# A graph layer on one core: slots of 511 rows in four blocks instead of 383 in three, and a longer gather list

## The chip, the cores and the metric

The kernel runs on one core of one Trainium2 chip. The metric is the device time of one execution in microseconds (us). Five engines with queues of their own work in it: TensorE (PE; its weight loads are listed apart as PEld), VectorE (DVE), ScalarE (ACT), GpSimd (POOL) and SyncE (SP), which only issues DMAs here. Before the change the median of three runs is 703.79 us (703.43 to 704.61).

## The reference

6250 nodes have 256 features each, 100,000 edges run from node `src` to node `dst` and are sorted by `dst`. Cut to what matters:

```python
theta_x = (x[dst] - x[src]) @ theta_w.T + theta_b
phi_x = x[src] @ phi_w.T + phi_b
e = relu(theta_x + phi_x)
out = segment_max(e, dst, num_segments=6250)     # nodes without edges: 0
return layernorm(x + out)
```

Since the maximum runs over the edges of one node, the part that depends on `dst` leaves the maximum: with B = x @ (phi_w − theta_w).T a node needs the largest B row of its sources, column by column; to it come x @ theta_w.T and the biases, then the relu, the sum with x and the normalisation.

## The kernel before, in words

**B.** PE computes B for all nodes in pairs of 128 rows (`b_of`, L782 to L794) and ACT writes it to `b_rows` in DRAM. `weights` holds both matrices, [:, :, 0] for B and [:, :, 1] for theta.

**Two parts.** The first 618 nodes (part 1) are served by gathers alone: 81 steps (`FIRST_STEPS`), in each of which GpSimd gathers one row of B for each of the 128 partitions by an indirect DMA (`gather`, L527 to L535), and DVE takes the running maximum (`run_steps`, L687 to L707; line L696). Steps go in groups of 8, on a ring of 5 tiles named `g`. The first two groups (`X_GROUPS`) gather rows of x and need no `b_rows`; the others wait for it. The other 5632 nodes (part 2) are 44 (`TILES`) in each partition, with room for 36 (`R`) edges each, their ranks.

**Slots.** The rows of B are cut into slots of 383 rows (`SLOT_ROWS`), two blocks of 128 (`KB` = 3 blocks with the last) and one of 127; the free row holds a very small value for "no edge here". There are 17 slots, of which the last has 122 rows and so one block. For each slot and node one edge is chosen whose source lies in the slot (`choice`, L1027 to L1055, on DVE, two slots at a time, int16 over `CHOICE_R` = 24 ranks); its row number within the slot goes to `chosen_rows` in DRAM (`wanted`). Rows are then fetched by products with one-hot matrices: for each slot and each chunk of 1024 nodes (`CHUNKS`, five of 1024 and one of 512), `make_hots` (L1144 to L1161) loads the row numbers to all partitions and builds one one-hot block of 128 x 1024 for each block of rows. ACT does it in two passes, |want − row| (L1157) and relu(1 − that) (L1160); DVE does a block in one (L1155): the first block in each slot's first chunk and, once `dve_hots` is set, the first in every chunk. `slot_halves` (L1099 to L1140) multiplies: B is split into two float32r terms (`slot_terms`, L1071 to L1095), each chunk has two halves of 128 features, each half blocks x 2 terms x 2 matmuls of 512 columns (L1120) into a PSUM tile of two banks, `ps_f`, of which there are three. ACT copies the halves of slot 0 into `acc` (L1132), DVE takes the maximum of `acc` and the halves of all other slots (L1134, the evictions).

**The list.** What the slots do not choose (a second edge of the same node and slot, and ranks past the 24th) is put into a list of 128 x 256 places (`LIST_CHUNK`): `list_pieces` (L1247 to L1322) marks the edges that are left, moves them to the front of each partition in 11 steps of DVE (L1278, L1288), stores them in `list_words` in DRAM, and reads them back by three indirect DMAs (`gather_run`, L540 to L544), so that each partition has 256 steps whatever node they belong to. Each step is a gather of `b_rows` (`gather_2`) and a maximum (L696) as in part 1; the last is a carry. The groups are stored to `maxima_2`, and at the end each node's maximum is gathered from there by its place (44 gathers).

**What sets the order.** GpSimd's gathers have a written order (`in_turn`). While the list is built, the loop at L1555 hands out by turns the groups of part 1 (even pieces) and parts of slots (odd pieces), with `AHEAD_OF_RUNS` chunks behind the store and one fewer behind the reads. In the list (L1606 to L1632) the steps of group i − 2 stand between the gathers of group i; every second gather waits for a step of DVE that lies 16 steps back (`hold`, L537). `halves_until` (L1601) spreads the slots' halves over the list, but for the last 10 chunks (`LAST_CHUNKS`), which come behind it. DVE's evictions are tied to the list's steps by order-only dependencies (L1139), so that both run in this order. Within these ties a scheduler places the instructions of each engine.

**The end.** `rows_of` (L1359 to L1420) handles the nodes in shares of 8, 4 and 2 tiles: theta's products, the transposed `acc`, the gathered maxima, relu, sum and normalisation. The first share stands between the last chunks of the last slot (L1657).

A `pause` of one iota of 160 elements stands behind each `gather_run` and behind the gather of the heads of part 1 (L544, L928). If a window, the list or a partition does not hold the data, `flags` makes the kernel run `general_path` behind the rest.

Of the kernel before, what the change touches and what calls it, by code (L numbers as in the profile page):

```python
# [39 lines left out]
FP = mybir.dt.float32  # L40
# [11 lines left out]
P = 128  # L52
# [17 lines left out]
PAUSE = 160  # L70
CHOICE_R = 24
# [11 lines left out]
LAST_CHUNKS = 10  # L83
LEAD = 2
STEPS_BITS = 3
OWN_LIST = 316
LIST_CHUNK = 256
# [348 lines left out]
def gnn_kernel(ctx: ExitStack, tc: tile.TileContext, x, src, dst, theta_w, theta_b, phi_w, phi_b, out):  # L436
# [14 lines left out]
    CW = 1024  # L451
# [4 lines left out]
    assert D == 2 * P and LEFT1 > 0 and OWN % 512 == 0 and TILES < 64 and P * T1 < E and WINDOW < E  # L456
    assert (P - 1) * T + 1 < E <= P * T and N < ID_MASK and P * T <= EDGES and E + 8 * P <= EDGES
    assert SLOT * NS <= slot_code(WORD - 1) < 1 << 15 and N < WORD and WORD << TABLE_BITS == 1 << 23 and SLOT == 1 << SLOT_BITS and P == 1 << P_BITS and SLOT_ROWS < SLOT and KB == 3 and ROWS == P - 1 and WINDOW <= 8 * P and OWN_LIST * P < 1 << 20
    BATCH_S = 2
    assert STEPS == 1 << STEPS_BITS and 3 * BATCH_S * CHOICE_R * TILES // 2 + TR <= 6 * WINDOW and LIST_CHUNK + 1 == LIST and LIST_CHUNK % STEPS == 0 and 3 * (BACK + LIST_CHUNK) <= WINDOW and BACK == R - 2 and CARRY_GROUPS * STEPS >= BACK and BACK + LIST_CHUNK <= OWN_LIST and R == 36 and CHOICE_R == 24 and OWN_LIST <= 512 and 1536 < TR <= 1536 + OWN_LIST  # L460
# [47 lines left out]
    pause = const.tile([P, PAUSE], FP, name="pause")  # L508
# [211 lines left out]
    weights = const.tile([P, KC, 2, D], FP, name="weights")  # L720
# [3 lines left out]
    with (  # L724
# [6 lines left out]
        w_in = prep.tile([P, 2, KC, D], FP, name="w_in")  # L731
        for i, w in enumerate((phi_w, theta_w)):
            nc.sync.dma_start(w_in[:, i], w.rearrange("(c p) k -> p c k", p=P))
        biases = prep.tile([P, 2, D], FP, name="biases")
        nc.vector.tensor_sub(w_in[:, 0], w_in[:, 0], w_in[:, 1])
        for i in range(2):
            for c in range(KC):
# [3 lines left out]
                weights_made = nc.vector.tensor_copy(weights[:, :, i, c * P : (c + 1) * P], ps[:, 0])  # L741
# [40 lines left out]
        def b_of(to, rows, kept=None):  # L782
# [6 lines left out]
            for h in range(n):  # L789
                for k in range(KC):  # L790
                    nc.tensor.matmul(  # L791
                        ps[:, h, :], x_t[:, h, k, :], weights[:, k, 0, :], start=(k == 0), stop=(k == KC - 1)
# [125 lines left out]
    def heads_1(capped):  # L918
# [4 lines left out]
        carried = work.tile([P, D], FP, name="carried", bufs=1)  # L923
# [4 lines left out]
        in_turn(iota(pause, 1, 0, 0))  # L928
# [13 lines left out]
    words, work_1, work_2, order = (table(n) for n in ("words", "work_1", "work_2", "order"))  # L942
# [5 lines left out]
    behind_in_order(iota(order, 1, 1, 0), windows_fetched[0], "runs ahead of the ranks")  # L948
# [78 lines left out]
    def choice(s0):  # L1027
# [71 lines left out]
    def slot_halves(s, c):  # L1099
# [13 lines left out]
        for h in range(KC):  # L1113
            ps = ps_fetch.tile([P, CW], FP, name="ps_f")
            ps = ps[:, :wide_of]
            n = blocks * PARTS
            for i in range(n):
                b, part = divmod(i, PARTS)
                for w in range(0, wide_of, 512):
                    one = nc.tensor.matmul(  # L1120
                        ps[:, w : w + 512],
                        terms[:, part, b, h * P : (h + 1) * P],
                        hot[:, b, w : w + 512],
# [6 lines left out]
            to = acc[:, h, begin : begin + wide_of]  # L1130
# [116 lines left out]
    def list_pieces():  # L1247
# [10 lines left out]
        nc.vector.tensor_tensor(up_to[:, 1:], node_ends(order), node_ends(before_it), op=ALU.subtract)  # L1258
# [7 lines left out]
        distance = order.bitcast(I32)  # L1266
# [37 lines left out]
        list_edges, second, third = (dst_w[:, i * n_run : (i + 1) * n_run] for i in range(3))  # L1304
# [54 lines left out]
    def rows_of(part, j0, n, ps_tile):  # L1359
# [18 lines left out]
        def piece(k):  # L1378
            w = min(2, n - k)
            if part == 2:  # L1380
                j = j0 + k
                if j % 4 == 0:
                    x_tiles[0] = kept_ring.tile([P, 4 * KC, P], FP, name="kept")
                    rows = x_columns[:, j * KC * P : (j + 4) * KC * P]
# [317 lines left out]
```

## Time and profile before

| | before |
|---|---|
| median of 3 runs | 703.79 us (703.43 to 704.61) |
| the profiled execution | 703.84 us, span 702.0 us, granted clock 0.97 |
| PE busy | 650.7 us (93%) |
| PEld busy | 532.1 us (76%) |
| DVE busy | 627.0 us (89%) |
| ACT busy | 513.2 us (73%) |
| POOL busy | 438.1 us (62%) |
| slot products (L1120) | 2156 matmuls, 508.1 us |
| list gathers (L528, list_src) | 256, 262.4 us |
| evictions (L1134) | 192, 216.4 us |

Times in rows of the profile are microseconds from the start of the span, unless a row gives a mean in ns. A row of a group of instructions has the line, the engine, the operation, tiles out<-in, shape, count, then busy time, mean ns of one, idle time of the engine ahead of them and what ended it. A row of the order of time has start, duration, engine, line, operation, and in brackets the idle time before it and what ended that. The span starts at the first and ends at the last instruction of the profiled execution.

### The profile page before, as it was taken

The page shows a single profiled execution, that of the slowest core. Times are in us where ns is not written, and L with a number is a line of the kernel's source. Part 1 is how long each engine was busy: PE and PEld are TensorE (multiplying, and loading weights), DVE is VectorE, ACT ScalarE, POOL GpSimd, SP SyncE. Part 2 cuts the span into 40 slices and gives each one's busy share as a digit, 9 for nine tenths or more (in the row PEclk, how much of TensorE's full clock was granted, in tenths as well). Part 3 has the DMA queues.
Part 4 walks back from the last instruction along what each step waited for, and adds up shares of the span by engine and source line. Part 5 has one row for each costly group of instructions (what it writes and reads, how often), then busy time and mean ns, then how long its engine had stood idle before and what let it go on. Part 6 is the DMA issues. An engine that isn't in the chain of part 4 may idle for free.

```text
span 702.0 us, 9583 instructions
## 1 busy us (share of the span) xinstructions
PE 650.7 (93%) x2908; PEld 532.1 (76%) x2908; DVE 627.0 (89%) x1200; ACT 513.2 (73%) x597; POOL 438.1 (62%) x424
## 2 busy tenths in 40 slices
PE   4899978879798999999999999999999999999991
PEld 3688866657577788888888888888888878888881
DVE  6999999999998778989889897889888898979996
ACT  1345668989888877868778786779877687863596
POOL 6800178888813757777777677777667776057720
PEclk9899989989999999999999999999999999999996
DMA  8898563656645747868697689788887776655775
GB/s 249 293 350 322 191 187 109 204 192 210 215 174 182 260 150 255 266 225 284 209 319 241 219 302 332 230 247 280 307 267 262 247 235 208 206 170 162 261 292 206
DMA packets 61308, 167.04 MB, mean 238 GB/s; under 512 B 11944, under 2 KB 21953, under 8 KB 55233
## 3 DMA queue, kind: packets, MB, share of 16 engines
q1 hardware_dynamic: 40005, 106.89, 43.9%
q0 software_dynamic: 18976, 52.35, 25.1%
q10 hardware_dynamic: 2268, 7.11, 2.8%
q8 instruction: 25, 0.41, 0.3%
q14 instruction: 34, 0.28, 0.1%
HBM read 102.94 MB, written 63.36 MB: 237 GB/s over the span
## 4 chain that ended last, share of the span: by engine, by line
PE 61%; DVE 16%; ACT 7%; POOL 6%; issue 5%; DMA 4%; ACTq 0%; SPq 0%; DVEq 0%; POOLq 0%
PE ps_f L1120 58%; POOL g L528 6%; DVE words L1005 2%; ACT hot L1157 2%; ACT x_f L1458 2%; ACT hot L1160 2%; DMA g<-b_rows,src 1%; DVE work L1002 1%; DVE g L696 1%; ACT squares L1443 1%; DVE wide L1038 1%; DVE x_f L1414 1%; PE ps_e L1400 1%; DMA dst_w<-in_dst_dram,window 1%; DVE g L1410 1%
## 5 line engine op out<-in xcount | busy, mean ns | idle before, releaser
L1120 PE MATMUL ps_f<-hot,terms 128*128 128x512 f32 x2156 | 508.1, 396 | 18.8 <-DVE hot L1155 10.5
L1120 PEld LDWEIGHTS ps_f<-hot,terms 128*128 128x128 f32 x2156 | 406.6, 190 | 113.8 <-ACT hot L1160 14.6
L528 POOL DMA_INDIRECT g<-b_rows,list_src x256 | 262.4, 1025 | 107.8 <-issue 52.2
L1157 ACT ACTIVATE hot<-want,minus_row 128x1024 fp32r<-128x1024 f16 (+1 forms) x214 | 219.3, 1074 | 99.1 <-PE ps_f L1120 98.9
L1134 DVE TENSOR_TENSOR acc<-acc,ps_f 128x1024 f32<-128x1024 f32 x192 | 216.4, 1129 | 49.7 <-PE ps_f L1120 47.8
L1160 ACT ACTIVATE hot<-hot 128x2048 fp32r<-128x2048 f32 (+2 forms) x102 | 188.8, 1851 | 2.4
L696 DVE SCALAR_TENSOR_TENSOR g<-g,caps 128x256 f32<-128x256 f32 x335 | 161.1, 481 | 1.7
L528 POOL DMA_INDIRECT g<-b_rows,src x65 | 92.3, 1420 | 66.5 <-DMA b_rows<-b_sb 47.1
L791 PE MATMUL ps_b<-weights,x_t 128*128 128x256 f32 x260 | 63.7, 400 | 7.6 <-ACT x_t L779 7.2
L528 POOL DMA_INDIRECT g<-maxima,place x44 | 42.2, 960 | 33.7 <-DMA maxima<-g 20.6
L791 PEld LDWEIGHTS ps_b<-weights,x_t 128*128 128x128 f32 x260 | 50.4, 200 | 16.7 <-ACT x_t L779 10.1
L1155 DVE TENSOR_SCALAR hot<-want,row_id 128x1024 fp32r<-128x1024 f16 x80 | 56.9, 712 | 0.0
L794 ACT COPY b_sb<-ps_b 128x512 f32<-128x512 f32 (+1 forms) x25 | 14.4, 579 | 30.8 <-PE ps_b L791 21.1
L1400 PE MATMUL ps_e<-weights,kept 128*128 128x256 f32 x144 | 34.0, 379 | 0.0
L1443 ACT ACTIVATE squares<-x_f,r 128x256 bf16<-128x256 f32 x47 | 23.2, 494 | 12.5 <-DVE r L1440 12.5
L1400 PEld LDWEIGHTS ps_e<-weights,kept 128*128 128x128 f32 x144 | 27.3, 190 | 3.6
L528 POOL DMA_INDIRECT g<-in_x_dram,src x16 | 21.1, 1320 | 5.4 <-issue 4.1
L779 ACT COPY x_t<-ps_xt 128x512 f32<-128x512 f32 (+1 forms) x33 | 18.3, 590 | 7.8 <-PE ps_xt L776 7.6
L1458 ACT ACTIVATE x_f<-x_f,r 128x256 f32<-128x256 f32 x40 | 20.6, 587 | 4.6 <-DVE r L1450 4.6
L1288 DVE COPY_PREDICATED work<-words,work 128x316 int32<-128x316 int32 (+9 forms) x11 | 18.2, 1659 | 0.0
L1414 DVE SCALAR_TENSOR_TENSOR x_f<-g,x_f 128x256 f32<-128x256 f32 x44 | 17.1, 423 | 0.3
L1038 DVE TENSOR_TENSOR wide<-wide 128x88 int16<-128x88 int16 (+5 forms) x45 | 16.2, 360 | 1.3
(273 smaller groups left out, 405.8 us busy)
## 6 DMA issues: line engine op xcount, KB each, us to landing
maxima<-g SPq DMA_DIRECT2D x41, 1024.0 KB
want<-chosen_rows SPq DMA_DIRECT2D x85, 256.0 KB
x_q<-in_x_dram SPq DMA_DIRECT2D x12, 512.0 KB
b_rows<-b_sb ACTq DMA_DIRECT2D x12, 512.0 KB
x_columns<-x_t SPq DMA_DIRECT2D x22, 256.0 KB
kept<-x_columns SPq DMA_DIRECT2D x11, 512.0 KB
raw<-b_rows SPq DMA_DIRECT2D x16, 256.0 KB
g<-b_rows,list_src POOLq DMA_INDIRECT x256, 4.9
```

The source lines that it names most:

```text
L528: one = nc.gpsimd.indirect_dma_start(out=to, out_offset=None, in_=table, in_offset=bass.IndirectOffsetOnAxis(ap=offsets, axis=0))
L696: one = nc.vector.scalar_tensor_tensor(g[:, k, :], last[part], caps[:, t : t + 1], g[:, k, :], op0=ALU.min, op1=ALU.max)
L791: nc.tensor.matmul(ps[:, h, :], x_t[:, h, k, :], weights[:, k, 0, :], start=(k == 0), stop=(k == KC - 1))
L1120: one = nc.tensor.matmul(ps[:, w : w + 512], terms[:, part, b, h * P : (h + 1) * P], hot[:, b, w : w + 512], start=(i == 0), stop=(i == n ...
L1134: one = nc.vector.tensor_tensor(to, to, ps, op=ALU.max)
L1155: nc.vector.tensor_scalar(hot[:, b, :], want, row_id[:, b : b + 1], None, op0=ALU.is_equal)
L1157: nc.scalar.activation(hot[:, b, :], want, AF.Abs, bias=minus_row[:, b : b + 1], scale=1.0)
L1160: nc.scalar.activation(apart, apart.bitcast(FP), AF.Relu, bias=1.0, scale=-1.0)
L1400: nc.tensor.matmul(a[:, i, :], x_t[:, 2 * i + c, :], weights[:, c, 1, :], start=False, stop=(i == w - 1 and c == KC - 1))
L1414: one = nc.vector.scalar_tensor_tensor(y, m[:, i, :], 0.0, y, op0=ALU.max, op1=ALU.add, accum_out=totals[:, i : i + 1])
L1443: nc.scalar.activation(squares, x_f[:, k, :], AF.Square, bias=mean[:, k : k + 1], scale=1.0, accum_out=var[:, k : k + 1])
L1458: nc.scalar.activation(x_f[:, k, :], x_f[:, k, :], AF.Identity, bias=mean[:, k : k + 1], scale=inv[:, k : k + 1])
```

## The change

Slots become 511 rows in four blocks (`KB` = 4): 13 slots, the last of 118 rows with one block. Chunks are 960 nodes wide (the last 832) and are multiplied as two pieces of half the width, each in a bank of its own. The choice runs over 20 ranks. With fewer slots and ranks more edges are left: the list has 312 steps and a carry, 40 groups instead of 33. Part 1 has 80 steps, 10 groups instead of 11. Ahead of the list the odd pieces hand out half a chunk instead of one, and 2 and 1 chunks instead of 3 and 2 stand behind the store and the reads. 9 chunks instead of 10 are kept for behind the list. The pauses are taken out. Several tiles change for room: B's weights move into a pool that is freed early, the table `order` is replaced by 44 values (`node_top`) and its other use goes to `before_it`, the third read of the list's words goes into `src_w`, and `carried` shares a tile with `tails`.

```diff
-AHEAD_OF_RUNS = 3
+AHEAD_OF_RUNS = 2
-FIRST_STEPS = 81
+FIRST_STEPS = 80
-LIST = 257
+LIST = 313
-KB = 3
+KB = 4
-PAUSE = 160
-CHOICE_R = 24
+CHOICE_R = 20
-LAST_CHUNKS = 10
+LAST_CHUNKS = 9
-OWN_LIST = 316
-LIST_CHUNK = 256
+OWN_LIST = 384
+LIST_CHUNK = 312
...
-    CW = 1024
+    CW = 960
...
         indirect(to, flat(table, 0, [[total, 1], [1, total]]), bass.IndirectOffsetOnAxis(ap=offsets, axis=1))
-        in_turn(iota(pause, 1, 0, 0))
...
-    weights = const.tile([P, KC, 2, D], FP, name="weights")
+    weights = const.tile([P, KC, D], FP, name="weights")
...
+        weights_b = prep.tile([P, KC, D], FP, name="weights_b")
...
         indirect(heads, maxima_1, in_offset=at_heads)
-        in_turn(iota(pause, 1, 0, 0))
...
-    behind_in_order(iota(order, 1, 1, 0), windows_fetched[0], "runs ahead of the ranks")
+    node_top = index.tile([P, TILES], FP, name="node_top")
+    behind_in_order(iota(node_top, R, R, 0), windows_fetched[0], "runs ahead of the ranks")
...
-        least(low, in_slot[:, :n, : 12 * W], in_slot[:, :n, 12 * W :])
-        least(low[:, :, : 6 * W], low[:, :, : 6 * W], low[:, :, 6 * W :])
-        least(low[:, :, : 3 * W], low[:, :, : 3 * W], low[:, :, 3 * W : 6 * W])
+        least(low, in_slot[:, :n, : 10 * W], in_slot[:, :n, 10 * W :])
+        least(low[:, :, : 5 * W], low[:, :, : 5 * W], low[:, :, 5 * W :])
+        least(low[:, :, : 2 * W], low[:, :, : 2 * W], low[:, :, 2 * W : 4 * W])
         least(low[:, :, :W], low[:, :, :W], low[:, :, W : 2 * W])
-        least(low[:, :, :W], low[:, :, :W], low[:, :, 2 * W : 3 * W])
+        least(low[:, :, :W], low[:, :, :W], low[:, :, 4 * W : 5 * W])
...
-            ps = ps_fetch.tile([P, CW], FP, name="ps_f")
-            ps = ps[:, :wide_of]
+            ps = ps_fetch.tile([P, 2, 512], FP, name="ps_f")
+            half = wide_of // 2
+            ps = ps[:, :, :half]
...
-                for w in range(0, wide_of, 512):
+                for w in range(2):
                     one = nc.tensor.matmul(
-                        ps[:, w : w + 512],
+                        ps[:, w, :],
                         terms[:, part, b, h * P : (h + 1) * P],
-                        hot[:, b, w : w + 512],
+                        hot[:, b, w * half : (w + 1) * half],
...
-        list_edges, second, third = (dst_w[:, i * n_run : (i + 1) * n_run] for i in range(3))
+        list_edges, second = (dst_w[:, i * n_run : (i + 1) * n_run] for i in range(2))
+        third = src_w[:, :n_run]
...
         elif i % 2 == 0:
             next_group_1(1)
         else:
-            fetch_parts(1)
+            fetch_half()
+            if len(groups_1) == 0 and i < 13:
+                fetch_half()
...
-    while halves_left[0] > 2 * (len(CHUNKS) - 1):
+    while halves_left[0] > 2 * (len(CHUNKS) - 2):
         fetch_half()
```

More of the change, by code (lines that the diff above doesn't have):

```diff
@@ L941, in gnn_kernel @@
     by_node = "p (j r) -> p j r"
-    words, work_1, work_2, order = (table(n) for n in ("words", "work_1", "work_2", "order"))
+    words, work_1, work_2 = (table(n) for n in ("words", "work_1", "work_2"))
     word = words.bitcast(I32)
@@ L1129, in slot_halves @@
                 hots_of[parts[0]] = make_hots(*parts[0])
-            to = acc[:, h, begin : begin + wide_of]
+            to = acc[:, h, begin : begin + wide_of].rearrange("p (w n) -> p w n", w=2)
             if s == 0:
```

30 lines of the change are left out of this document (15 added, 15 removed).

## The prediction

> **What bounds the kernel now.** I read the busy shares first, then the stages in a table of time windows, then the order of GpSimd's instructions at the stage borders, last the waits. Columns of a window: its length, then busy time and count for PE, PEld, DVE, ACT, POOL, the clock, DMA share, GB/s.
>
> ```profile
> PE 650.7 (93%) x2908; PEld 532.1 (76%) x2908; DVE 627.0 (89%) x1200; ACT 513.2 (73%) x597; POOL 438.1 (62%) x424
> ```
>
> ```profile
> 62.60:118.40 55.80, 48.98 (x229) 40.55 (x228) 53.38 (x119) 38.22 (x55) 27.76 (x23) 0.92 0.58 191
> 118.40:224.80 106.40, 90.07 (x363) 70.87 (x362) 102.82 (x182) 92.13 (x98) 68.82 (x51) 0.93 0.59 191
> 224.80:597.70 372.90, 372.49 (x1640) 303.92 (x1639) 325.06 (x539) 291.74 (x254) 270.54 (x265) 1.00 0.77 254
> 644.00:687.30 43.30, 43.20 (x234) 37.77 (x234) 40.63 (x150) 32.43 (x104) 22.69 (x24) 1.00 0.78 276
> ```
>
> By share PE is the bound: in the list stage (224.8 to 597.7) it is busy 372.5 of 372.9. Before the list DVE is the full one (102.8 of 106.4) and PE has holes. GpSimd at 62% seems free. But its busy time leaves out 0.30 us between two gathers:
>
> ```profile
> 635.86 0.95 POOL L528 DMA_INDIRECT g<-maxima,place  x1 [0.30 <-issue]
> 637.11 0.95 POOL L528 DMA_INDIRECT g<-maxima,place  x1 [0.30 <-issue]
> ```
>
> A gather that nothing disturbs starts 1.25 us after the last one. These are the gathers by stage (window, busy, count) and where the stages begin and end:
>
> ```profile
> 83.90:196.00 112.10, 92.30 (x65) 0.89 0.58 183
> 224.80:597.70 372.90, 268.15 (x262) 1.00 0.77 254
> ...
> 195.06 0.95 POOL L528 DMA_INDIRECT g<-b_rows,src  x1 [0.31 <-issue]
> 212.66 1.10 POOL L521 DMA_INDIRECT dst_w<-list_words,run_start  x1 [16.66 <-DMA list_words<-work]
> 224.80 1.14 POOL L528 DMA_INDIRECT g<-b_rows,list_src  x1 [7.91 <-DVE list_src L1314]
> 254.48 1.21 POOL L528 DMA_INDIRECT g<-b_rows,list_src  x1 [4.76 <-DVE g L696]
> 596.77 1.02 POOL L528 DMA_INDIRECT g<-b_rows,list_src  x1 [0.30 <-issue]
> 618.35 0.94 POOL L528 DMA_INDIRECT g<-maxima,place  x1 [20.57 <-DMA maxima<-g]
> ```
>
> In the list stage GpSimd issues 264 (these 262 and the two for the heads). At 1.25 that is 330 us; the 262 last 268.15, 19 us over 0.95 each; the remaining 24 of the 372.9 us are waits for DVE. So GpSimd fills 94% of the list stage: **PE and GpSimd are nearly level there**, PE a little ahead of it as the bound. That is the reading on which the forecast rests.
>
> **The change part by part.**
>
> *Slots.* 17 slots hold 16 × 3 + 1 = 49 blocks of rows, 13 hold 12 × 4 + 1 = 49. The one-hot products run over the same 49 × 2 terms × 2 halves × 5632 columns, but as 2352 matmuls (1960 of 480 columns, 392 of 416) instead of 2156 of 512. A dense stretch of the chain gives the pace, and a group row the weight loads:
>
> ```profile
> 247.07 126.13 PE ps_f L1120 x552
> L1120 PEld LDWEIGHTS ps_f<-hot,terms 128*128 128x128 f32 x2156 | 406.6, 190 | 113.8 <-ACT hot L1160 14.6 <-issue 11.9 <-ACT g L794 1.1
> ```
>
> 126.13 / 552 = 228.5 ns. By columns 480 take 214 ns; 416 would take 186, but a weight load takes 190. Sum 1960 × 0.214 + 392 × 0.190 = 494 us against 2156 × 0.2285 = 493: +1 us. No shorter float32r product is in the trace; the bounds are this and 228.5 ns each, +45 us. I take +1, since the weight loads at 190 ns leave room below 214. PE's work therefore does not fall; only its holes can close.
>
> *Evictions* (DVE) go from 192 to 144, the columns from 16 × 2 × 5632 to 12 × 2 × 5632:
>
> ```profile
> L1134 DVE TENSOR_TENSOR acc<-acc,ps_f 128x1024 f32<-128x1024 f32 x160 | 194.8, 1218 | 48.9 <-PE ps_f L1120 47.2
> L1134 DVE TENSOR_TENSOR acc<-acc,ps_f 128x512 f32<-128x512 f32 x32 | 21.6, 681 | 0.8 <-PE ps_f L1120 0.7
> ```
>
> 216.4 us fall to 120 × 1.15 + 24 × 1.02 = 162 us, −54. In the list stage this is beside PE and GpSimd and earns nothing; some 20 of the 48 fewer lie before the list, about −10 us there.
>
> *One-hots.* ACT makes what DVE leaves: of four blocks three in the list stage, and all four before it (but in a slot's first chunk).
>
> ```profile
> L1157 ACT ACTIVATE hot<-want,minus_row 128x1024 fp32r<-128x1024 f16 x178 | 195.2, 1145 | 81.9 <-PE ps_f L1120 81.8
> L1160 ACT ACTIVATE hot<-hot 128x2048 fp32r<-128x2048 f32 x67 | 128.5, 1918 | 1.5
> L1160 ACT ACTIVATE hot<-hot 128x3072 fp32r<-128x3072 f32 x13 | 36.1, 2774 | 0.3
> ```
>
> The second pass costs (2774 − 1918) = 0.86 us per 1024 columns and 0.2 fixed; the first about 1.02 per block of 960. A chunk costs ACT 3 × 1.02 + 2.6 = 5.7 us in the list stage against 32 × 0.214 = 6.9 us of PE: hidden, with less room than now. Before the list it is 4 × 1.02 + 3.4 = 7.5 us, more than PE's 6.9 (now 6.2 against 5.5). There PE stays behind ACT, and 16 chunks ahead of the list in the written order, for 22 now, are about the same work for ACT.
>
> *Choice.* One undisturbed batch of two slots, less the terms (about 0.87 of DVE) in it:
>
> ```profile
> 89.64 0.77 DVE L1034 TENSOR_SCALAR wide<-padded 128x1056 int16<-128x1056 int16 x2
> ...
> 95.48 0.95 DVE L1092 TENSOR_TENSOR terms<-raw,terms 128x768 fp32r<-128x768 f32 x1
> 96.35 0.80 DVE L1034 TENSOR_SCALAR wide<-padded 128x1056 int16<-128x1056 int16 x2
> ```
>
> 6.71 − 0.87 = 5.85 us; eight such and a half one (3.6) are 50.4. With 20 of 24 ranks, fixed parts kept, about 5.0; six and a half one (3.0) are 33. So −17 us of DVE, all on its full stretch.
>
> *Start of the list.* DVE's work ahead of it falls by 17 + 10 and a few small ones, about 29 us: alone it would have the list's words stored at 181 instead of 210. But their three gathers stand behind the first part's on GpSimd's queue. Those begin at 83.9, when b_rows is written (unchanged), and end at 196.0. One gather fewer and less choice beside them: 192. ACT's pace puts the chunks that DVE evicts before the words near there too. From the first words gather to the first list gather there are now 12.1 us. So the list starts at about **205** instead of 224.8. Bounds: 184, if the 30 us by which those 65 gathers exceed 0.95 go with the DVE work; 224, if ACT holds it all. I take 205, since the longest of these stretches lie beside list steps that stay:
>
> ```profile
> 118.73 3.68 DVE L1250 SCALAR_TENSOR_TENSOR work<-padded,unused 128x1584 f32<-128x1584 int16 x1
> 118.80 4.45 POOL L528 DMA_INDIRECT g<-b_rows,src  x1 [0.30 <-issue]
> ```
>
> *The list itself.* 312 gathers for 256, with the 8 others 320: × 1.25 = **400 us**. To it comes the stretching:
>
> ```profile
> 303.58 0.75 DVE L1155 TENSOR_SCALAR hot<-want,row_id 128x1024 fp32r<-128x1024 f16 x1
> 303.93 1.21 POOL L528 DMA_INDIRECT g<-b_rows,list_src  x1 [0.40 <-DVE g L696]
> ...
> 224.80:597.70 372.90, 51.14 (x72) 1.00 0.77 254
> ```
>
> (the last row: DVE's hots in the stage). 19 us over 72 hots is 0.27 each, as in the pair above. About 57 hots of 960 give 14 us; by gathers it would be 320 × 0.073 = 23. I take 19. Beside these rows: the Trainium skill, "SBUF — State Buffer", section "Who interferes with whom", says that a VectorE operation in a two-port mode holds the pair of ports it shares with GpSimd for its whole length and GpSimd blocks fully. By that, each of the 57 hots could cost up to its own 0.71 us, 40 us in place of 19; the pair of rows shows less, since a gather is hit only on part of its length.
>
> Waits for DVE: the first, 4.76 us, comes when the 16 gathers' lead is used up before DVE starts on the list; with four-block chunks waiting ahead of it, 8 us. Later ones go, because GpSimd is the later one: 320 × 1.31 = 419 us, against some 393 of slot products and 7 of others left for PE in that stage. DVE then waits for rows in its fixed order, the evictions queued behind these steps wait too, and PE for its PSUM tiles. The last gather ends at 205 + 400 + 19 + 8 = **632** instead of 597.8.
>
> *The end.* Now DVE trails the last gather by 17.5 us (its lead, unused):
>
> ```profile
> 614.91 0.43 DVE L694 TENSOR_TENSOR g<-g,heads 128x256 f32<-128x256 f32 x1
> g<-b_rows,list_src POOLq DMA_INDIRECT x256, 4.9
> ```
>
> If GpSimd is last, only the landing remains (4.9 us from issue) and two steps: 5 us. From the last step (615.3) to the end are 86.7 us: slots left over, then the shares at PE's pace. 15 halves instead of 17 are left and PE is up to three ahead: 5 us less, 81.7. The gathers of the places follow 1.25 apart with some 7 us to spare.
>
> At nothing I cost: the pauses taken out (0.3 us each, GpSimd's idle time covers three of them, 1 us if not), the smaller iota (GpSimd idles until 83.9), wider list tiles and rows' casts (under 0.3 us each beside PE), the loads of rows in the same three pieces.
>
> **Sum.** 632 + 5 + 81.7 = 718.7 of span; the profiled execution took 703.84 for a span of 702.0, so **720.5**. It lies 0.05 over the median of 703.79, so I compare directly: +16.7 us.
>
> **Rivals.**
> 1. *List early, faster: 699.* Place: the first part's gathers, 83.9 to 196. Their 30 us of stretching fall with the DVE work, the list starts at 184, all else as above. For it: the choice runs beside 24 of them. Against: scan, compaction and first list step remain, and ACT's 7.5 us chunks. It decides from a start before 188.
> 2. *Start unmoved, 739.* Four-block hots on ACT hold PE and with it DVE's ordered evictions; the list starts at 224. For it: ACT 92.1 of 106.4 us busy there. Against: ACT's sum there does not grow.
> 3. *Matmuls cost per instruction, 733 to 745.* +45 us on PE makes it the bound again: its work left at 205 is then some 530 us with the shares and the end.
> 4. *A draw, within 1.4 us of 703.8:* start near 195 and no wait for DVE.
> 5. *The list does not fit* and the general path runs behind the rest. Counted on the inputs, 39,751 rows are left for 128 × 312 = 39,936 places and at most 376 in a partition for 384: as good as excluded.
>
> **Chances.** Forecast (708 to 730) 0.60; rival 1 0.18; rival 2 0.11; rival 3 0.05; draw 0.05; rival 5 0.01. Faster by over 0.2% (what a measurement tells here from no change) 0.18, within it 0.05, slower 0.77. Range 699 to 737: rival 1 at its edge, most of rival 2 out.
>
> **What would show it.** The first gather by the list near 205; the last near 632, 320 of them 1.3 us apart; in that stage PE below 97% and GpSimd's long waits for DVE gone, DVE's list steps waiting for rows instead. Evictions 144, about 162 us. Wrong it is if PE still is busy throughout the list stage, if the list starts before 188, or if the 480-column matmuls are paced at 228 ns.

## Result, and the profile after

The changed kernel takes **737.01 us** (median; 733.21 to 743.86), the kernel before 704.18 (703.43 to 704.61): a ratio of 1.048, 95% interval 1.040 to 1.056. The prediction said slower, at 720.5 us within 699 to 737. The sign was right. The size was not: half of the loss had not been forecast, and the time lies 0.01 us beyond the upper end of the range. Two later executions in a slow state (1097.3 us of the kernel before, at a granted clock of 0.56, and 935.2 us of the kernel without halves ahead, at 0.66) are left out of every comparison. The profiled execution of the changed kernel took 743.86 us for a span of 742.1, about 7 us more than the median; the terms below are that execution's.

From the page of the changed kernel: the span, the chain that ended last, and the costliest groups (busy time and mean of one, then idle time and what ended it).

```profile
span 742.1 us, 9929 instructions
...
DMA 26%; PE 24%; DVE 20%; issue 11%; ACT 10%; POOL 8%; SPq 0%; DVEq 0%; POOLq 0%; ACTq 0%
...
L1120 PE MATMUL ps_f<-hot,terms 128*128 128x480 f32 (+1 forms) x2352 | 524.3, 384 | 47.2 <-DVE acc L1134 24.5
...
L526 POOL DMA_INDIRECT g<-b_rows,list_src x312 | 318.4, 1021 | 121.4 <-issue 60.3
...
L1134 DVE TENSOR_TENSOR acc<-acc,ps_f 128x960 f32<-128x960 f32 x144 | 161.9, 1127 | 44.0 <-PE ps_f L1120 43.9
L526 POOL DMA_INDIRECT g<-b_rows,src x64 | 97.1, 1517 | 70.2 <-DMA b_rows<-b_sb 51.1
```

The chain no longer runs mostly through PE, which held 61% of it before. Its two largest pieces are now the landing of list rows and the slot products, 20% each. The evictions are 144 where there were 192. Now GpSimd's queue about the list (start, duration, instruction, and in brackets its idle time ahead and what ended it):

```profile
209.39 1.44 POOL L526 DMA_INDIRECT g<-b_rows,list_src  x1 [6.11 <-DVE dst_w L1317]
...
232.61 0.95 POOL L526 DMA_INDIRECT g<-b_rows,list_src  x1 [0.30 <-issue]
253.49 1.07 POOL L526 DMA_INDIRECT g<-b_rows,list_src  x1 [19.93 <-DVE g L693]
...
652.99 0.94 POOL L526 DMA_INDIRECT g<-b_rows,list_src  x1 [0.30 <-issue]
662.95 0.95 POOL L526 DMA_INDIRECT g<-maxima,place  x1 [9.02 <-DMA maxima<-g]
```

The first gather by the list comes 15.4 us earlier than before (209.39 for 224.80). Then GpSimd uses up its lead, stands for 19.93 us, and goes on at 253.49. Before, the same wait was 4.76 us and ended at 254.48. So the list really gets going at almost the **same moment** in both kernels, and all but 1.0 us of the earlier start is waited away. From there to the last gather's end it is 400.45 us; before, 343.3. That is 57.1 us more for 56 gathers more, which at 1.25 us would be 70: the waits that GpSimd had all through this stage before, some 19 us in all, are gone but for 2, while the gathers are stretched by some 4 us more. Behind the last gather's end the changed kernel needs 88.2 us for 104.2, so the spans differ by 40.1 us.

What that wait is for stands on VectorE's queue. Here is the stretch in which its first list step comes, first of the changed kernel, then of the kernel before:

```profile
240.67 1.16 DVE L1134 TENSOR_TENSOR acc<-acc,ps_f 128x960 f32<-128x960 f32 x1 [2.31 <-PE ps_f L1120]
244.56 1.15 DVE L1134 TENSOR_TENSOR acc<-acc,ps_f 128x960 f32<-128x960 f32 x1 [2.11 <-PE ps_f L1120]
248.01 1.15 DVE L1134 TENSOR_TENSOR acc<-acc,ps_f 128x960 f32<-128x960 f32 x1 [2.29 <-PE ps_f L1120]
249.08 0.48 DVE L693 SCALAR_TENSOR_TENSOR g<-g,caps 128x256 f32<-128x256 f32 x1
```

```profile
246.89 1.22 DVE L1134 TENSOR_TENSOR acc<-acc,ps_f 128x1024 f32<-128x1024 f32 x1 [1.50 <-PE ps_f L1120]
248.03 0.48 DVE L696 SCALAR_TENSOR_TENSOR g<-g,caps 128x256 f32<-128x256 f32 x1
```

In the written order the first list step stands behind slot halves. Between 204 and 249 us VectorE evicts fourteen of them. The two halves of a chunk come 3.45 us apart (16 matmuls of 0.212 us make 3.4; before, halves of three blocks came 2.72 us apart), and to the first half of the next chunk it is 3.9 to 4.0 us. There TensorE follows ScalarE, which makes the four-block hots without a pause, 7.39 us a chunk:

```profile
225.89 4.04 ACT L1157 ACTIVATE hot<-want,minus_row 128x960 fp32r<-128x960 f16 x4
229.96 3.41 ACT L1160 ACTIVATE hot<-hot 128x3840 fp32r<-128x3840 f32 x1
233.28 4.04 ACT L1157 ACTIVATE hot<-want,minus_row 128x960 fp32r<-128x960 f16 x4
```

```profile
233.43 7.20 PE L1120 MATMUL ps_f<-hot,terms 128*128 128x480 f32 x32 [0.23 <-ACT hot L1160]
```

The first list step is at 249.08 us, and was at 248.03, although VectorE had less to do: from 118.4 us to this step it is busy 90.6 us for 120.5. TensorE's slot work ahead of the step is about the same (517 matmuls recorded, of up to 480 columns, for 497 of 512), but in that stretch it stands idle 27.1 us for 16.7. Of these, 18.3 us are three waits for an eviction (8.58, 2.37 and 7.32 us), where the kernel before has one of 0.2 us. The last of the three, on TensorE's queue and then on VectorE's:

```profile
205.72 18.85 PE L1120 MATMUL ps_f<-hot,terms 128*128 128x480 f32 x80 [7.32 <-DVE acc L1134]
```

```profile
204.08 0.55 DVE L1311 COPY_PREDICATED dst_w<-words,dst_w 128x346 int32<-128x346 int32 x1 [6.82 <-DMA dst_w<-list_words,run_start]
204.52 1.14 DVE L1134 TENSOR_TENSOR acc<-acc,ps_f 128x960 f32<-128x960 f32 x1
```

The eviction that TensorE needs stands on VectorE's queue behind the list's words, for which VectorE waits 6.82 us. So what VectorE saved went into longer waits on the way, and equal slot work alone does not explain the equal moment. No run tries the evictions in another place.

The rest of the list stage, from the waits (who waited for whom: us in total, times, longest) and from the stretches before and after the end of that wait (length; PE, PEld, DVE, ACT and POOL busy with counts; granted clock, DMA share, GB/s):

```profile
DVE g L693 <- DMA g<-b_rows,list_src: 77.9, 58, 5.2
...
POOL g L526 <- DVE g L693: 38.5, 59, 19.9
```

```profile
209.39:253.49 44.10, 42.44 (x198) 36.76 (x198) 23.27 (x50) 39.61 (x29) 18.68 (x19) 0.99 0.53 169
253.49:653.94 400.45, 383.39 (x1771) 335.16 (x1769) 297.24 (x506) 315.56 (x246) 308.10 (x301) 0.97 0.78 253
```

After 253.49 it is as forecast: GpSimd waits for VectorE hardly at all (of its 38.5 us, 19.9 are the first wait, and most of the others are the 0.3 us that stand between any two gathers anyway), VectorE waits for rows 58 times, and PE is 95.7% busy where it was 99.9%.

### The profile page after: what moved, and what is told of

It reads as the page before. It is cut to its first block, busy times and chain, and to the rows that moved or that the text cites. A ratio compares the mean times of both kernels' runs of the same rounds, so it can differ in the third digit from the quotient of the medians.

```text
span 742.1 us, 9929 instructions
## 1 busy us (share of the span) xinstructions
PE 662.9 (89%) x3102; PEld 575.4 (78%) x3102; DVE 576.4 (78%) x1158; ACT 544.9 (73%) x588; POOL 492.4 (66%) x473
## 4 chain that ended last, share of the span: by engine, by line
DMA 26%; PE 24%; DVE 20%; issue 11%; ACT 10%; POOL 8%; SPq 0%; DVEq 0%; POOLq 0%; ACTq 0%
DMA g<-b_rows,list_src 20%; PE ps_f L1120 20%; POOL g L526 8%; DVE g L693 5%; ACT hot L1157 4%; ACT hot L1160 3%; DVE words L1004 2%; DVE acc L1134 2%; PE ps_e L1401 2%; DMA g<-b_rows,src 2%; ACT x_f L1459 1%; DVE work L1001 1%; DMA x_q<-in_x_dram 1%; DVE wide L1037 1%; ACT acc L1132 1%
## 5 line engine op out<-in xcount | busy, mean ns | idle before, releaser
L1120 PE MATMUL ps_f<-hot,terms 128*128 128x480 f32 (+1 forms) x2352 | 524.3, 384 | 47.2 <-DVE acc L1134 24.5
L1120 PEld LDWEIGHTS ps_f<-hot,terms 128*128 128x128 f32 x2352 | 452.0, 194 | 113.0 <-DVE acc L1134 24.2
L526 POOL DMA_INDIRECT g<-b_rows,list_src x312 | 318.4, 1021 | 121.4 <-issue 60.3
L1157 ACT ACTIVATE hot<-want,minus_row 128x960 fp32r<-128x960 f16 (+1 forms) x235 | 237.3, 1077 | 105.1 <-PE ps_f L1120 102.3
L693 DVE SCALAR_TENSOR_TENSOR g<-g,caps 128x256 f32<-128x256 f32 x390 | 187.8, 482 | 96.1 <-DMA g<-b_rows,list_src 77.9
L1160 ACT ACTIVATE hot<-hot 128x2880 fp32r<-128x2880 f32 (+2 forms) x78 | 200.5, 2571 | 1.8
L1134 DVE TENSOR_TENSOR acc<-acc,ps_f 128x960 f32<-128x960 f32 x144 | 161.9, 1127 | 44.0 <-PE ps_f L1120 43.9
L526 POOL DMA_INDIRECT g<-b_rows,src x64 | 97.1, 1517 | 70.2 <-DMA b_rows<-b_sb 51.1
L790 PE MATMUL ps_b<-weights_b,x_t 128*128 128x256 f32 x260 | 61.1, 390 | 3.8 <-ACT x_t L778 3.6
L790 PEld LDWEIGHTS ps_b<-weights_b,x_t 128*128 128x128 f32 x260 | 49.3, 195 | 12.2 <-ACT x_t L778 6.0
L1155 DVE TENSOR_SCALAR hot<-want,row_id 128x960 fp32r<-128x960 f16 (+1 forms) x59 | 42.6, 721 | 0.0
L778 ACT COPY x_t<-ps_xt 128x512 f32<-128x512 f32 (+1 forms) x33 | 18.6, 587 | 11.0 <-PE ps_xt L775 7.9
```

The source lines that it names most:

```text
L526: one = nc.gpsimd.indirect_dma_start(out=to, out_offset=None, in_=table, in_offset=bass.IndirectOffsetOnAxis(ap=offsets, axis=0))
L693: one = nc.vector.scalar_tensor_tensor(g[:, k, :], last[part], caps[:, t : t + 1], g[:, k, :], op0=ALU.min, op1=ALU.max)
L790: nc.tensor.matmul(ps[:, h, :], x_t[:, h, k, :], weights_b[:, k, :], start=(k == 0), stop=(k == KC - 1))
L1120: one = nc.tensor.matmul(ps[:, w, :], terms[:, part, b, h * P : (h + 1) * P], hot[:, b, w * half : (w + 1) * half], start=(i == 0), stop=( ...
L1134: one = nc.vector.tensor_tensor(to, to, ps, op=ALU.max)
L1155: nc.vector.tensor_scalar(hot[:, b, :], want, row_id[:, b : b + 1], None, op0=ALU.is_equal)
```

## The experiments

All ratios are to the kernel before on the same chip. The runs came on three chips, four kernels on each. On the chip of the first four kernels the kernel before took 800.3 us, on that of the next four 798.8, on that of the last four 704.3, as in the first measurement. Whether the chips themselves make this difference is not shown. The first two are like one another but are two chips, which the expectations call "the second chip" as if they were one. Absolute times in the first expectations are for a chip of 704 us; what counts of them is the difference.

**Taking the wait away, on the chip of 704 us.** The control is the changed kernel itself.

> The changed kernel again, as the control for the next three on their chip. On the first chip 737.0 us (1.048 of before), on the second 860.6 (1.079). Both theories: between 1.04 and 1.085 of the kernel before, whichever chip it is.

Measured: 742.5 us, ratio 1.054 (1.052 to 1.056). Its trace has the first wait again:

```profile
257.49 1.07 POOL L526 DMA_INDIRECT g<-b_rows,list_src  x1 [18.73 <-DVE g L693]
```

First experiment: the six extra halves ahead of the list's first step go into the list stage.

```diff
-AHEAD_OF_RUNS = 2
+AHEAD_OF_RUNS = 0
```

> The changed kernel with none of the six extra slot halves that stand in the written order ahead of the list's first step (AHEAD_OF_RUNS 0 in place of 2). With 1, four halves less, the second chip showed the first wait of the gathers 16.2 us where the unmodified kernel had 31.7, and 11.0 us less in all. Theory (the list effectively begins when VectorE reaches its first list step, behind the halves at TensorE's pace of 3.45 us each; the gathers' own start does not matter): 6 x 3.45 = 21 us earlier first step, first wait nearly gone where it was 19.9, last gather and time 14 to 21 us earlier than the unmodified kernel on the same chip. Rival (TensorE sets the list stage too, 95% busy; what is taken from ahead of the list is paid in it): within 4 us of the unmodified kernel, with more waits of GpSimd for VectorE in the stage.

Measured: 721.0 us, ratio 1.022 (1.019 to 1.025), so 21.5 us less than the control. VectorE's queue at its first list step, GpSimd's at the list's two ends, and the stage as one stretch:

```profile
223.48 1.15 DVE L1134 TENSOR_TENSOR acc<-acc,ps_f 128x960 f32<-128x960 f32 x1 [0.68 <-PE ps_f L1120]
...
225.19 0.46 DVE L693 SCALAR_TENSOR_TENSOR g<-g,caps 128x256 f32<-128x256 f32 x1
```

```profile
208.85 1.44 POOL L526 DMA_INDIRECT g<-b_rows,list_src  x1 [6.21 <-DVE dst_w L1317]
...
632.26 0.95 POOL L526 DMA_INDIRECT g<-b_rows,list_src  x1 [0.30 <-issue]
```

```profile
208.85:633.20 424.35, 417.95 (x1967) 367.36 (x1965) 322.21 (x557) 351.68 (x273) 327.14 (x320) 1.00 0.78 257
```

The first list step comes 23.9 us earlier than in the first trace of the changed kernel, the first gather where it was (208.85), and no gather in between waits: no idle time between two of them is longer than 0.35 us. The last one ends at 633.2 us for 653.9. The theory holds, at the upper edge of its 14 to 21 us. The rival (TensorE takes it back) falls, with one reservation: TensorE is now 98.5% busy in the stage, so little more of this kind is to be had there.

Second experiment: the halves stay, but the gathers may run ahead of VectorE as far as the ring of five row tiles allows.

```diff
     def hold(k):
-        return used[-2] if held[0] and k % 2 == 0 else None
+        return None
```

> The changed kernel without the hold once more. On the second chip it took 59 us more than with it: the first gathers did run on without a wait of 30 us, but later TensorE had spells of up to 25 us with one matmul in 0.7 to 1.4 us, and gathers waited 8 to 31 us for the stores of row tiles. Theory A (the loss is that chip's: its TensorE falls into slow spells): on a chip without such spells it is 10 to 20 us faster than the unmodified changed kernel. Theory B (gathers that run ahead of VectorE cost the others something on any chip): slower than the unmodified one by over 5 us here too.

Measured: 720.2 us, ratio 1.021 (1.018 to 1.024), 22.3 us less than the control, a little more than the 10 to 20 us of theory A, which holds on this chip. VectorE's first list step is where it was, and GpSimd's one wait is short:

```profile
248.52 0.48 DVE L693 SCALAR_TENSOR_TENSOR g<-g,caps 128x256 f32<-128x256 f32 x1
```

```profile
265.50 0.95 POOL L526 DMA_INDIRECT g<-b_rows,list_src  x1 [4.02 <-DVE acc L1134]
...
635.45 0.95 POOL L526 DMA_INDIRECT g<-b_rows,list_src  x1 [0.30 <-issue]
```

The two experiments take the wait away from its two sides, an earlier first step and a longer lead, and give the same 21 to 22 us. So that wait costs the kernel about its full length, and it is GpSimd's queue, not VectorE's first step as such, through which it reaches the end. The forecast already held 8 us of it; the 12 us beyond are the larger part of the gap between forecast and result.

**The same with the hold gone, on a chip of 799 us.** Here it went the other way.

> The changed kernel once more, beside the next three on the same chip, so that their differences are taken against it. On the first chip it took 737.0 us against 704.2 before (ratio 1.048). On the second chip the two kernels with more and fewer gathers bracket it: 915.6 us less 36 gathers, and 817.5 us plus 39, at 1.31 us for each, both put it at 868.5 us there, a ratio of 1.085 to before. Theory (GpSimd's queue sets the changed kernel, TensorE nearly sets the one before): the ratio is 1.05 on a chip like the first and 1.07 to 1.09 on one like the second. Rival (the end is set by TensorE's products in both): the ratio stays at 1.048 on every chip.

Measured: 860.6 us, ratio 1.079 (1.072 to 1.086): inside what the theory gave for a chip of this kind.

> The changed kernel without the hold on GpSimd's gathers: a gather no longer waits for VectorE's step 16 back, and only the ring of five row tiles (40 gathers) limits it. Theory (the first wait of the list, 19.9 us where 8 was forecast, delays GpSimd's queue and with it the end): the wait at the list's start goes, since 40 gathers from 209.4 us on last to 260 us and VectorE's first list step begins at 249 us; the last gather ends 15 to 20 us earlier and the time falls by 13 to 20 us against the unmodified changed kernel on the same chip. Rival (VectorE or TensorE sets the end of the list and GpSimd only waits for it): within 3 us of the unmodified one. Second rival (gathers ahead of VectorE's work lengthen each other, by the shared port and by landings): the gathers' mean rises from 1021 ns by over 40 ns and half of the gain or more is lost.

Measured: 919.4 us, ratio 1.148 (1.142 to 1.155), 58.8 us *more* than the control. None of the three expectations holds: the gathers' mean was 1000 ns, so they did not lengthen each other. TensorE's idle time ahead of slot products that nothing in the profile ends was 107.0 us for 45.0 in the control's trace. These 62 us are about the loss, so I put it to TensorE's spells, which the last section shows. Why it falls into such spells more without the hold, and on this chip, wasn't found out; the same kernel is 22 us faster than its control on the chip of 704 us.

**The length of the list.** On the chip of 800 us, where no control ran; I set these beside the control of the like chip (860.6), so a few us are uncertain.

```diff
             halves_until((i - LEAD) * STEPS + k + 2)
+        if i == 4:
+            spare = work.tile([P, KC, P], FP, name="capped", bufs=1).rearrange("p k n -> p (k n)")
+        if i >= 4:
+            gather(spare, b_rows, list_src[:, i : i + 1])
         list_store(i - LEAD)
```

> The changed kernel with one more gather behind each list group from the fifth on, 36 in all, of rows that nobody reads; PE, DVE and ACT do the same work as before. Theory (GpSimd sets the list): 36 x 1.32 = 47 us more, 784 +- 8. Rival (PE or DVE sets it, GpSimd has its busy share of 77% there and so room): under 10 us more, 737 to 747.

Measured: 915.6 us, ratio 1.146 (1.136 to 1.156); about 55 us more, 1.53 for each of 36 gathers that nobody reads, at the upper edge of the 47 +- 8 expected.

The other way round, the last step of each list group keeps the row before it and its gather is gone, 39 in all (those rows are left out of the maxima):

```diff
-            gather_2(g, i * STEPS, k, min(k + 2, LIST_CHUNK - i * STEPS))
+            gather_2(g, i * STEPS, k, min(k + 2, STEPS - 1, LIST_CHUNK - i * STEPS))
...
-caps[:, t : t + 1], g[:, k, :], op0=ALU.min, op1=ALU.max
+caps[:, t : t + 1], last[part] if part == 2 and k == STEPS - 1 else g[:, k, :], op0=ALU.min, op1=ALU.max
```

> The changed kernel without the gather of each list group's last step, 39 fewer; the step itself stays and takes the row of the step before it a second time, so DVE's, PE's and ACT's work is the same (the maxima lack these rows). Theory: 39 x 1.32 = 51 us less on GpSimd, of which about 27 us can be had before PE, whose holes in the list stage sum to that, sets the time: 703 to 716. Rival (the time lies with PE's 196 additional matmuls or with ACT): 732 to 738.

Measured: 817.5 us, ratio 1.025 (1.017 to 1.034); about 43 us less, 1.10 for each. That is more than the 21 to 34 us at which TensorE was expected to stop the gain. Between these two, which did run on one chip, lie 98.1 us for 75 gathers: **1.31 us each**. In their profiled executions the list stage differs by 99.4 us: 92.0 are the gathers with their gaps (1.23 each), 7.4 are waits. The rivals (no more than 10 us for 36 more, 5 for 39 fewer) fall. One reservation stays: TensorE's idle time that nothing in the profile ends is 81.2 us with the gathers added and 25.6 with them taken out, and whether that follows from the longer list or adds to it is not shown. The pair did not run on the chip of 704 us.

The kernel before, with 29 such gathers more:

> The kernel before with the same additional gather behind each list group from the fifth on, 29 in all. Theory (PE and GpSimd nearly level there, GpSimd with 24 us of waits for DVE and a lead of 16 gathers): 29 x 1.32 = 38 us more on GpSimd, of which 24 fill the waits and a part of the rest uses up the lead of some 17 us: 704 to 718. Rival 1 (GpSimd has room by its busy share of 72%): 704 +- 1.5. Rival 2 (GpSimd already sets the list before): 742.

Measured: 833.4 us, ratio 1.045 (1.036 to 1.054): 33.1 us more, 1.14 each. My theory of slack on GpSimd in the kernel before fell on this chip, and rival 2 (38 us more) comes nearest: GpSimd had 72.9 us of waits for VectorE's list steps, and the added gathers still cost nearly their full length. Behind a first wait of 14.5 us these waits come mostly in pieces of 1 to 4 us; I take it that a gather more at another moment doesn't use them, which no run shows. Whether it is the same on a chip of 704 us, where the waits were 38.9 us, wasn't run.

**Single parts of the change.** Fewer halves ahead, in a smaller step, on the chip of 800 us:

```diff
-AHEAD_OF_RUNS = 2
+AHEAD_OF_RUNS = 1
```

> The changed kernel with AHEAD_OF_RUNS = 1 in place of 2: one chunk instead of two behind the store of the list's words, none instead of one behind the reads; the four halves go into the list stage. Theory (GpSimd sets the list; its first wait of 19.9 us comes from 14 halves of some 3.45 us that DVE must evict ahead of its first list step): the wait falls by about 4 x 3.45 = 14 us to some 6 us, the last list gather ends about 14 us earlier, 737 becomes 723 to 725. Rival (PE sets the list, the wait is only lead that is given back later): 735 to 738.

Measured: 849.6 us, ratio 1.066 (1.057 to 1.076) against the control's 1.079 on its like, 11 us less where 12 to 14 were expected. The first wait is 16.19 us for 31.65. The direction is the theory's, but the intervals overlap; the clear evidence is the run with 0 above.

The choice over 24 ranks again, in the changed kernel:

```diff
-CHOICE_R = 20
+CHOICE_R = 24
```

(with the pairs of the minimum's tree 12, 6, 3, 1, 1 ranks wide as before)

> The changed kernel with the choice over 24 ranks again, as before; the list keeps its 312 steps (it has 39,475 rows with 24 ranks, 39,751 with 20). Theory (the 17 us of VectorE that the shorter choice saves lie beside GpSimd's part-1 gathers, which set the list's start): at most 3 us slower than the unmodified changed kernel on the same chip, first list gather within 3 us. Rival (VectorE's preparation sets the list's start): the first list gather 6 to 17 us later, and the time 6 to 17 us longer.

Measured: 853.4 us, ratio 1.067 (1.059 to 1.076), not slower than the control on the same chip. Its first list gather came 9.1 us later (213.16 for 204.03) and its first wait was 18.6 us shorter (13.03 for 31.65), since VectorE's first list step came 11.1 us earlier (244.40 for 255.48), which I can't explain. That the gathers' start would not move was wrong. That the time would not grow was right, and it fits the reason found above: the list waits for VectorE's first step whenever its gathers begin.

Chunks of 960 columns in two pieces, alone, in the kernel before:

```diff
-    CW = 1024
+    CW = 960
...
-            ps = ps_fetch.tile([P, CW], FP, name="ps_f")
+            ps = ps_fetch.tile([P, 2, 512], FP, name="ps_f")
+            half = wide_of // 2
...
-                for w in range(0, wide_of, 512):
+                for w in range(2):
```

> The kernel before with chunks of 960 columns in two pieces of 480 alone (last chunk 832 in two of 416, where it was 512 in one piece); slots, ranks, list and all else as before. Theory (a matmul costs by its columns: 480 at 214 ns, 416 at 190 ns, against 228 ns for 512): 17 slots then have 1,044 us of columns at the same rate and as many more instructions as the last chunk needs, TensorE's work in the products rises by 1 to 5 us and the time by 0 to 6 us. Rival (a matmul costs by the instruction, 228 ns or more whatever the columns): TensorE's products rise by a ninth or so of the last chunk's share, some 45 us, and the time by 30 to 45 us.

Measured: 796.8 us, ratio 0.997 (0.994 to 1.001): no difference to be told from nothing, so the theory holds and the cost by instruction falls. (The 1,044 us of columns in the expectation are a slip; by the prediction's sum the products are 494 us.) The products' matmuls of this kernel, on its chip, and of the unmodified kernel before on the chip of 704 us; the busy times are the sums to compare, while the means count matmuls that overlap and are not their pace:

```profile
L1121 PE MATMUL ps_f<-hot,terms 128*128 128x480 f32 (+1 forms) x2352 | 524.2, 381 | 82.1 <-DVE acc L1135 41.1
```

```profile
L1120 PE MATMUL ps_f<-hot,terms 128*128 128x512 f32 x2156 | 508.1, 396 | 18.8 <-DVE hot L1155 10.5 <-ACT hot L1160 7.6 <-ACT g L794 0.5
```

**A version that could beat both.** The kernel before with what the change shortens and the list does not pay for:

```diff
-AHEAD_OF_RUNS = 3
+AHEAD_OF_RUNS = 2
...
-FIRST_STEPS = 81
+FIRST_STEPS = 80
...
-CHOICE_R = 24
+CHOICE_R = 22
...
-        in_turn(iota(pause, 1, 0, 0))
```

(both pauses, and the pairs of the minimum's tree cut to fit 22 ranks)

> The kernel before with those parts of the change that need no longer list, cut to fit: slots of 383 rows in three blocks and 256 list steps stay, chunks of 1024 stay; choice over 22 ranks, 80 first gathers, no pauses, AHEAD_OF_RUNS 2 in place of 3. Theory (the list effectively begins at VectorE's first list step; TensorE and GpSimd are about level in its stage): the first step comes 8 to 15 us earlier, but what is not done ahead of the list is paid in it, so 0 to 6 us faster than before. Rival (TensorE alone sets the kernel before): within 1.5 us of before, or slower by what waits come in new.

Measured: 703.56 us for 704.32, ratio 0.9985 (0.9972 to 0.9998). It is the fastest kernel of this study, by less than 1 us, and that lies inside both expectations, so it does not decide between them. The wait near the list's start is gone and the last gather ends 2.9 us earlier (594.9 for 597.8), but that hardly reaches the end. Its chain fits that: PE holds 61% of it, as before.

```profile
PE 61%; ACT 9%; DVE 5%; issue 4%; POOL 4%; DMA 2%; DVEq 0%; POOLq 0%
```

## Why the prediction was right or wrong

By the terms of its sum, against the profiled execution (span 742.1; the sum gave 718.7):

- *Start of the list*, 205: measured 209.4 (213.8 in the second trace). The last gather of the first part ended at 199.5 for 192; 4.4 us.
- *Gathers*, 320 × 1.25 = 400: measured 320, with 319 pitches of 1.25 between them, 399. Right.
- *Stretching*, 19: measured about 24 beyond 0.945 us each; 5 us. The prediction's estimate by the Trainium skill ("SBUF — State Buffer", section "Who interferes with whom"), a block for the whole length of a hot, was up to 40. The trace agrees in that gathers beside a hot are longer, but not by so much: some 70 of the gathers lie beside a hot and take 1.10 us in the mean, 0.15 over the undisturbed 0.945. Whether the hots run in a two-port mode no run shows. The hots are not all of it: 14 other gathers, beside the split of B into its terms (L1091), take 1.40 us in the mean.
- *First wait*, 8: measured **19.9**, and 0.9 of other waits. This is the step that failed, and 12.8 of the 23.4 us by which the span exceeds the sum.
- *VectorE behind the last gather*, 5 us to the end of the steps, and *the end*, 81.7: measured 88.2 together, for 86.7.

The step that failed is the first wait, and it failed in its logic before its size. The prediction said that "16 chunks ahead of the list in the written order, for 22 now, are about the same work for ACT"; for TensorE, 16 chunks of four blocks and 22 of three are nearly the same too. It also said that VectorE's list steps stand in a fixed order with the evictions, and so behind these chunks. It nevertheless moved the list to 205 by following GpSimd's queue and the fall of VectorE's work (about 29 us forecast, 30 measured), and did not ask when VectorE reaches its first list step. For the wait, "with four-block chunks waiting ahead of it, 8 us" stood without a sum. The trace has the step at 249.1 for 248.0: eighteen gathers by the list and one for the heads, from 209 on, are used up at 233.6, the first step comes 15.5 us later, and the held gather then still waits for a second one. As the lines above show, the step did not have to stay exactly there; that it moved by only 1 us came with waits of TensorE for evictions that nobody had forecast.

The two kernels that lack the wait take 721.0 and 720.2 us, against a forecast of 720.5. That they meet it so closely is luck: the forecast held 8 us of wait, and without any its sum gives 712.5. The rest is the later start, the stretching and the end, 4.4, 5 and 1.5 us in the first trace.

The five rivals:

- 1, *the list early*: no. The first part's gathers became longer in the mean (1517 ns for 1420), not shorter.
- 2, *start unmoved, 739*: nearest in number, and half right in mechanism. Products hold VectorE's ordered evictions and with them its list steps, and over the last 25 us ahead of the first step ScalarE's hots do pace them (7.39 us a chunk, 7.5 forecast). But the gathers' own start did move, and TensorE's longest waits ahead of the list were for evictions, not for hots.
- 3, *matmuls cost by the instruction*: no. They go at 0.212 us for 480 columns (forecast 0.214), and the chunks of 960 alone cost nothing.
- 4, *a draw*: no; the first list gather came after 195, and VectorE did make it wait.
- 5, *the list does not fit*: no, it fits.

What was right: GpSimd's queue becomes what sets the list stage (from 253.49 on it waits 2 us in all, and removing its first wait shortens the kernel by that wait); evictions 162 us (161.9); PE below 97% in the stage (95.8); VectorE's list steps waiting for rows. The parts costed at nothing stay unseparated; nothing in the trace points at them. Of the 48 evictions fewer, 12 lay ahead of the first list step (20 for 32), where some 20 were put ahead of the list. The spread of the changed kernel is not explained either: 733 to 744 us in its first four executions, 741 to 744 in the later ones, for 703 to 705 and 703 to 707 before.

## What to carry to other kernels

Where two queues meet in a written order, the later of the two starts sets the stage, so move both or count on neither: here GpSimd's start came 15 us earlier and 1 us was gained, until either the six halves ahead of VectorE's first step went or the gathers' lead grew. When a resource is relieved on average, list what stands *in order* ahead of the first use, before and after, and who waits for whom on the way: here VectorE had 30 us less to do and its first list step did not come earlier. And what is added to the queue that sets a stage is paid in that queue's units: 56 gathers more at 1.25 us are 70 us, of which 57 showed in the stage here because old waits went. A low busy share does not show that a queue has room: on the chip of 800 us each gather added to the kernel before cost 1.14 us, although GpSimd waited 72.9 us there.

## What the runs showed of the hardware that was not expected

**A stall of TensorE cost more than its length.** TensorE about 399 us in the changed kernel, and the clock in the 5.5 us after it:

```profile
391.93 3.71 PE L1120 MATMUL ps_f<-hot,terms 128*128 128x480 f32 x16
399.51 9.71 PE L1120 MATMUL ps_f<-hot,terms 128*128 128x480 f32 x32 [3.87 <-DVE acc L1134]
```

```profile
399.50:405.00 5.50, 5.49 (x14) 4.59 (x15) 5.50 (x9) 0.00 (x0) 4.28 (x5) 0.50 0.71 199
405.00:409.00 4.00, 4.00 (x20) 3.49 (x19) 3.89 (x8) 3.15 (x4) 3.09 (x4) 0.99 0.97 267
```

After 3.87 us of waiting the granted clock is 0.50 for some 5 us: 14 matmuls in 5.5 us, where 20 go in the next 4.0. At the usual 0.212 us it would have been 26, so the stall costs 3.87 us and about 2.5 more. The Trainium skill ("TensorE: Matmul & The Clock Gate", section "What's actually happening") says that the array's clock falls to half after an idle window of about 3.4 us and returns after a busy one; this row agrees.

**On the two slower chips TensorE has spells at far below half its pace.** In the changed kernel without the hold, on the chip of 799 us, TensorE's queue read:

```profile
243.77 0.56 PE L1120 MATMUL ps_f<-hot,terms 128*128 128x480 f32 x1 [2.03 <-issue]
246.57 0.56 PE L1120 MATMUL ps_f<-hot,terms 128*128 128x480 f32 x1 [2.24 <-issue]
249.37 0.56 PE L1120 MATMUL ps_f<-hot,terms 128*128 128x480 f32 x1 [2.24 <-issue]
251.47 0.56 PE L1120 MATMUL ps_f<-hot,terms 128*128 128x480 f32 x1 [1.54 <-issue]
253.57 0.56 PE L1120 MATMUL ps_f<-hot,terms 128*128 128x480 f32 x1 [1.54 <-issue]
```

One matmul is recorded in 2.1 to 2.8 us, waiting for nothing that the profile shows, where the usual pace is 0.212. The granted clock, 0.50 from 240 to 256 us, would account for a factor of two only. Some records may be missing, but VectorE's next eviction also came 25.9 us after the last. The starts stand apart by multiples of 0.70 us. On the chip of 800 us the changed kernel with one chunk ahead shows the same (starts at 195.08, 197.18 and 199.28 us). The unmodified changed kernel on the chip of 799 us has such a spell too, 15 matmuls recorded in 12.1 us, with VectorE busy for 1.4 and ScalarE for 4.5 of them:

```profile
400.00:424.90 24.90, 24.89 (x120) 22.07 (x118) 19.96 (x43) 18.83 (x19) 19.41 (x19) 1.00 0.77 260
424.90:437.00 12.10, 6.22 (x15) 3.23 (x15) 1.38 (x4) 4.48 (x4) 9.36 (x10) 0.84 0.57 193
```

No stall of TensorE stands ahead of this one: the 120 matmuls before it follow one another without a gap. Its granted clock over the span is 0.901 for 0.957 in the control on the chip of 704 us, and GpSimd's waits in the list are some 84 us for 20, the first alone 31.65. How much of that is such spells was not separated, and what sets them off stays open. For the study it means that a difference found on one chip, the 59 us lost by the kernel without the hold, need not have the same sign on another.
